# Selective scan on one core: products with C moved one unit behind their scans, and GpSimd's share of them spread from pairs to every fourth unit

## The chip, the cores and the metric

One core of a Trainium2 chip runs the whole kernel in one launch. The metric is the time of the launch on the device in microseconds (us); the number given is the median of three runs. The engines of the core are named as the profile names them: PE (TensorE; PEld is its weight load), DVE (VectorE), ACT (ScalarE), POOL (GpSimd) and SP (SyncE, which issues nearly all DMAs here).

## The reference, cut to what matters

The input is `x`, 8 images of 96 channels and 64 x 64 pixels, so 4096 tokens each. Layer 0 is a group normalisation and a Mamba block; layer 1 is linear attention (no softmax) and a feed-forward net with rounded numbers. The change touches the Mamba block's selective scan, with 192 inner channels and 16 states:

```
delta = softplus(dt @ dt_proj_w.T + dt_proj_b)
dA    = exp(delta[..., None] * A)
dBu   = delta[..., None] * Bm[:, :, None, :] * u[..., None]
h_t   = dA_t * h_{t-1} + dBu_t            # 4096 steps in order
y_t   = sum over the 16 states n of h_t[:, n] * C_t[n]
y     = (y + u * D) * silu(z);  out = y @ out_proj_w.T
```

## The kernel before, in words

**Chunks and units.** The images are worked in four pairs, each in 8 chunks of 512 tokens: 32 chunks, in order. A chunk's scan is cut into 24 units (`NU`), numbered u = 0 to 23. Eight units belong to one of three channel blocks j; within these, two units (b = 0, 1) belong to each of four groups of states g. `where(u)` gives (j, g, b). One unit covers 128 partitions and two halves h of 512 tokens.

**What a unit needs.** POOL makes dBu as `dbu` (`products_b`, L659), three units ahead (`AHEAD`; four buffers). ACT makes exp(delta A) as `da` in PSUM (`decay`, L681; two buffers), for the next unit, each half emitted right behind the scan of the same half of this unit. DVE runs two scans into `hs` (L741; three buffers of `hs`). Then `hs` is multiplied by C into `pr`. In 18 of 24 units DVE does it (L763), reading C from PSUM tile `cc`, where PE has spread it over the partitions (`rows_c`, L671; two buffers). In the six units of `POOLED` = (4, 5, 12, 13, 20, 21) POOL does it (`pooled`, L770), reading C from an SBUF tile `c`. All six have g = 2, so one load of `c` per chunk serves them: four DMAs of 128 KB, issued in unit 23 of the chunk before (`rows`, L643). Last, PE adds up the states of a pair of units into `y` (`sums`, L695), and once per block j DVE multiplies `y` by silu(z) (`gate`, L709). As the kernel before stands, the sums of the pair 20, 21 are never issued.

**What lies around the scan.** The rest of the work is cut into steps of Python generators, which a table written out by hand (`STEPS`) places in the units. `P` is the projection, convolution and delta of a later chunk, `E` the output projection, two layer norms and Gram matrix of the chunk before, `F0` and `F1` the attention and feed-forward net of a chunk 9 back, for the two images of the pair, `W` the attention's weights, `G` the group statistics of the next pair. F steps therefore run from chunk 9 on. `F1` begins in unit 8 of a chunk and has its layer norm around unit 3 of the next, so its norm meets units 2 and 3 in chunks 10 to 31.

**What sets the order.** Every engine works through its instructions in the order in which the program emits them. In `unit` that order is: POOL's product of the unit before, if it is one of `POOLED`; a copy of the last state; `rows_c` of the next unit; sums; `now("norms")`, which emits POOL's part of a layer norm (L412, L131, L132, L414) whose statistics (L406, L408) DVE made in an earlier step; the unit's first steps; `products_b`; the scans with the decays; `now("others")` (POOL's casts L1011 and others); gate; the unit's second steps; and DVE's product. `normalise` (L420, ACT) comes in the step after the norm's statistics. In unit 10 (`SILU`) ACT also makes `da` of unit 12 ahead, into other banks, and then runs two Silu over 128 x 1536 with changes of the activation table (L492, L493).

**SP.** Its DMAs go out in program order, each after the DMA eight places before it has landed. In unit 0 it spreads du and dl of block 1 over the partitions (`spread`, L634): four DMAs of 256 KB each. Around them lie the two stores of `t1d` (L883) and the load of `xr` (L822).

Of the kernel before, what the change touches and what calls it, by code (L numbers as in the profile page):

```python
# [16 lines left out]
NS = 16  # L17
NJ = 3
NG = 4
# [2 lines left out]
NK = T // 128  # L22
HID = 384
RANK = 6
POOLED = (4, 5, 12, 13, 20, 21)
POOLED_G = 2
SILU = 10
ROWS_B = (16, 18, 20, 22)
AHEAD = 3
# [36 lines left out]
def tile_mamba_linear_attention_ffn(  # L66
# [474 lines left out]
    def first_p(s, after):  # L541


        rstd, nmr = gn[0]
        xt = x_next.pop((0, 0))
        u = p1.tile([C, 2, T + 3], F32, tag="u", name="u")
        nc.scalar.activation(
            u[:, 0, :], xt[:, 0, :], AF.Identity, bias=nmr[:, 0:1], scale=rstd[:, 0:1]
        )
        nc.vector.tensor_scalar(  # L550
            u[:, 1, :], xt[:, 1, :], rstd[:, 1:2], nmr[:, 1:2], ALU.mult, ALU.add
        )
        for b in range(2):
            nc.gpsimd.memset(u[:, b, 0:3], 0.0)
        load_x(*after)
        xm = s["xm"] = p2.tile([128, NJ, T], F32, tag="xm", name="xm")
        zs = s["zs"] = p2.tile([128, NJ, T], F32, tag="zs", name="zs")
        banks = ("mp", "mE", "mF")
        for j in range(NJ):
            ps = psum(banks[j])  # L560
            for k in range(4):
                for b in range(2):
                    nc.tensor.matmul(
                        ps[64 * b : 64 * b + 64, :], lhsT=wk[:, k, 64 * j : 64 * j + 64],
                        rhs=u[:, b, k : k + T], start=(k == 0), stop=(k == 3),
                    )
            nc.scalar.activation(xm[:, j, :], ps, AF.Silu, bias=cb[:, j : j + 1])

        def proj_z(j, bank):
            ps = psum(bank)  # L570
            for b in range(2):
                nc.tensor.matmul(
                    ps[64 * b : 64 * b + 64, :], lhsT=wz[:, 64 * j : 64 * j + 64],
                    rhs=u[:, b, 3 : T + 3], start=True, stop=True,
                )
            nc.scalar.activation(zs[:, j, :], ps, AF.Silu)

        proj_z(0, "cc")
        proj_z(1, "cc")
        dbl = p1.tile([C, T], F32, tag="dbl", name="dbl")  # L580
        ps = psum("y")
        for j in range(NJ):
            nc.tensor.matmul(
                ps[0:C, :], lhsT=xpT[:, j, :], rhs=xm[:, j, :],
                start=(j == 0), stop=(j == NJ - 1),
            )
        proj_z(2, "cc")
        nc.vector.tensor_copy(dbl, ps[0:C, :])
        bd = s["bd"] = dram.tile([4 * NS, T], F32, tag="bd", name="bd")
        nc.sync.dma_start(bd, dbl[32:96, :])  # L590
        rows_b(s, 0)
        delta = p1.tile([128, NJ, T], F32, tag="delta", name="delta")
        for j in range(NJ):
            pd = psum(banks[j])
            nc.tensor.matmul(
                pd, lhsT=dtT[:, j, :], rhs=dbl[0 : 2 * RANK, :], start=True, stop=True
            )
            nc.scalar.activation(delta[:, j, :], pd, AF.Softplus, bias=dtb[:, j : j + 1])
            ld = s["ld", j] = dram.tile([128, T], F32, tag=f"ld{j}", name="ld")
            nc.scalar.dma_start(ld, delta[:, j, :])  # L600
            du = p2.tile([128, T], F32, tag="du1", name="du")
            nc.vector.tensor_mul(du, delta[:, j, :], xm[:, j, :])
            lu = s["lu", j] = dram.tile([128, T], F32, tag=f"lu{j}", name="lu")
            nc.sync.dma_start(lu, du)
            if not j:
                for to in ("du", "dl"):
                    s[to, 0] = p2.tile([128, 4, T], F32, tag=to, name=to)
                for b in range(2):
                    for n in range(NG):
                        for to, of, queue in (("du", "lu", nc.sync), ("dl", "ld", nc.scalar)):  # L610
                            queue.dma_start(
                                s[to, 0][32 * n : 32 * n + 32, 2 * b : 2 * b + 2],
                                s[of, 0].rearrange("(q e) t -> e q t", e=32)[
                                    :, 2 * b : 2 * b + 2
                                ],
                            )

        cs = s["cs"] = p2.tile([128, T], F32R, tag="cs", name="cs")
        nc.vector.tensor_copy(cs[64:96], ps[64:96, :])
        nc.vector.tensor_sub(cs[96:128], dbl[64:96], cs[64:96].bitcast(F32))  # L620
        rows_b(s, 1)
        rows(s, "c", 2 * NS, POOLED_G)
        rows_b(s, 2)
        rows_b(s, 3)

# [12 lines left out]

    def rows(s, to, of, g):

        t = s[to, g] = p2.tile([128, 2, T], F32, tag=to, name=to, bufs=NG if to == "b" else 1)
        for n in range(NG):
            nc.sync.dma_start(  # L643
                t[32 * n : 32 * n + 32],
                s["bd"][of : of + 2 * NS].rearrange("(b n) t -> n b t", b=2)[NG * g + n]
                .unsqueeze(0)
                .to_broadcast([32, 2, T]),
            )

    def rows_b(s, g):  # L650
        rows(s, "b", 0, g)

    def where(u):
        return u // (2 * NG), (u // 2) % NG, u % 2
# [8 lines left out]

    def rows_c(s, u):
        j, g, b = where(u)
        if u in POOLED:
            return
        if ("low", 0) in s:
            settle(s["low", 0])
        cc = s["cc", u] = ps_all.tile([128, T], F32, tag="cc", name="cc", bufs=2)  # L670
        nc.tensor.matmul(  # L671
            cc, lhsT=sel[64:128, g, b], rhs=s["cs"][64:128, :], start=True, stop=True
        )
# [37 lines left out]
    def unit(s, prev, nxt, first, u, steps):  # L711
        def at(v):
            return (s, v) if v < NU else (nxt, v - NU)


        if u - 1 in POOLED:
            pooled(s, u - 1)
        if u:
            nc.scalar.copy(state["new"][:, u - 1, :], s.pop(("hs", u - 1))[:, :, T - 1])  # L719
        else:  # L720
            if prev is not None:
                nc.scalar.copy(state["new"][:, NU - 1, :], prev.pop(("hs", NU - 1))[:, :, T - 1])
            state["last"] = state.get("new")
            state["new"] = p2.tile([128, NU, 2], F32, tag="state", name="state")
        to, v = at(u + 1)
        if to is not None:
            rows_c(to, v)
        if u - 3 in POOLED and u % 2 == 0:
            sums(s, u - 3)
        if u % 2 == 0 and (u or prev is not None) and (u - 1) not in POOLED:  # L730
            sums(s if u else prev, (u or NU) - 1)
        now("norms")
        steps(u, 0)
        to, v = at(u + AHEAD)
        if to is not None:
            products_b(to, v)
        hs = s["hs", u] = p2.tile([128, 2, T], F32, tag="hs", name="hs", bufs=3)
        dbu = s.pop(("dbu", u))
        to, v = at(u + 1)
        for h in range(2):  # L740
            nc.vector.tensor_tensor_scan(  # L741
                hs[:, h, :], s.pop(("da", u, h)), dbu[:, h, :],
                0.0 if first else state["last"][:, u, h : h + 1], ALU.mult, ALU.add,
            )
            if to is not None:
                decay(to, v, h)
        now("others")

        new = u % (2 * NG) == 1
        if new and u > 1:  # L750
# [6 lines left out]
        steps(u, 1)  # L757
        if new:
            skip(s, u // (2 * NG))
        if u in POOLED:  # L760
            return
        pr = s["pr", u] = p2.tile([128, 2, T], F32, tag="pr", name="pr", bufs=4)
        nc.vector.tensor_mul(  # L763
# [1 line left out]
        )  # L765

    def pooled(s, u):
        j, g, b = where(u)
        pr = s["pr", u] = p2.tile([128, 2, T], F32, tag="pq", name="pr")
        nc.gpsimd.tensor_mul(  # L770
            pr, s["hs", u], s["c", g][:, b, :].unsqueeze(1).to_broadcast([128, 2, T])
        )


# [337 lines left out]
    with tc.manual_schedule():  # L1112
# [5 lines left out]
        for i, (p, c) in enumerate(chunks):  # L1118
# [4 lines left out]
            def steps(u, part):  # L1123
                if part == 0:
                    if u in (0, 2 * NG):
                        spread(s, 1 + u // (2 * NG))
                    if nxt is not None and u == 18:
                        spread(nxt, 0)
                    if nxt is not None and u in ROWS_B:
                        rows_b(nxt, ROWS_B.index(u))  # L1130
                    if nxt is not None and u == NU - 1:
                        rows(nxt, "c", 2 * NS, POOLED_G)
                for name in (STEPS[u] + "|").split("|")[part].split():
                    step(name, i)

# [3 lines left out]
    for kind in list(waiting):  # L1139
        now(kind)  # L1140
        del waiting[kind]
    s = slots[N - 1]
    sums(s, NU - 1)
    gate(s, NJ - 1)
    rest = [(p, c, b) for p in range(NP) for c in range(NCH) for b in range(2)]
# [81 lines left out]
```

## Time and profile before

| what | value |
|---|---|
| median of 3 runs (lowest, highest) | 3166.31 us (3162.42, 3171.55) |
| span of the profiled execution | 3160.5 us |
| the median less that span | 5.8 us |
| DVE busy | 2935.2 us (93%), 4265 instructions |
| POOL busy | 2840.7 us (90%), 1921 instructions |
| PE, ACT busy | 2469.6 us (78%), 2263.9 us (72%) |
| DMA traffic | 443.75 MB, 140 GB/s on average |
| mean time from chunk to chunk, chunks 1 to 8, 10 to 30 | 88.1 us, 93.9 us |

The profile is of one execution; its span runs from the first instruction to the last, and 5.8 us of the median time lie around it. A line such as `L741 DVE TENSOR_TENSOR_SCAN hs<-da,state,dbu` names the source line, the engine, the operation, what it writes and what it reads. In a timeline the first two columns are the start and the time taken, both in us from the span's start; xN is N instructions of one kind merged, and a bracket gives the engine's idle time before and who ended it. A chunk's start is here the start of its first scan; for the chunk that starts at 1606.80 the units start at 0, 3.7, 7.8, 12.75, 16.4, 18.8 and 21.7 us after that.

### The profile page before, as it was taken

The numbers are of one execution on the slowest core, as the hardware profiler recorded it, in microseconds if no ns is written. First come the engines' busy times: TensorE is split into PE (matmuls) and PEld (weight loads), VectorE is DVE, ScalarE is ACT, GpSimd is POOL, SyncE is SP. The second block draws the span as 40 slices with busy tenths as digits, with TensorE's granted clock in tenths as the row PEclk, the third lists the DMA queues.
The fourth block names the chain that finished last, engine by engine and source line by source line (L and its number), as shares of the span: only waits on it lengthen the run. The fifth ranks groups of instructions, "written<-read, shape, count | busy, mean of one in ns | idle before, by whom it ended". The sixth has DMA issues, their size and how long they took to land. (4 is left out here: it accounts for less than half of the span.)

```text
span 3160.5 us, 35127 instructions
## 1 busy us (share of the span) xinstructions
PE 2469.6 (78%) x9450; PEld 928.7 (29%) x9450; DVE 2935.2 (93%) x4265; ACT 2263.9 (72%) x4360; POOL 2840.7 (90%) x1921
## 2 busy tenths in 40 slices
PE   6787787878787777777777778777888778887777
PEld 2122222222222223222233323222323222332344
DVE  4999999999999999999999999999999999999945
ACT  3666666667677777777777777777877777777656
POOL 2999999999999999999999999999999999999955
PEclk8677777787778888888888877898888888877668
DMA  6655556665555667555667555567565466755322
GB/s 149 152 122 137 134 156 152 160 150 135 141 143 135 138 162 175 146 129 125 141 164 170 141 146 125 137 157 170 146 148 127 124 144 162 169 132 134 95 70 73
DMA packets 253037, 443.75 MB, mean 140 GB/s; under 512 B 37605, under 2 KB 45990, under 8 KB 252838
## 3 DMA queue, kind: packets, MB, share of 16 engines
q1 hardware_dynamic: 247846, 439.40, 56.9%
q10 hardware_dynamic: 4992, 2.11, 0.3%
q8 instruction: 74, 1.21, 0.2%
q14 instruction: 125, 1.02, 0.1%
HBM read 349.11 MB, written 92.27 MB: 140 GB/s over the span
## 5 line engine op out<-in xcount | busy, mean ns | idle before, releaser
L659 POOL TENSOR_TENSOR dbu<-du,b 128x1024 f32<-128x1024 f32 x768 | 1804.6, 2371 | 112.6 <-DVE hs L741 65.5
L741 DVE TENSOR_TENSOR_SCAN hs<-da,state,dbu 128x512 f32<-128x512 f32 x1290 | 1573.5, 1265 | 25.6 <-ACT da L681 24.6
L681 ACT ACTIVATE da<-dl,aneg 128x512 f32<-128x512 f32 x1474 | 1000.6, 688 | 665.4 <-DVE hs L741 644.2
L763 DVE TENSOR_TENSOR pr<-hs,cc 128x1024 f32<-128x1024 f32 x576 | 698.7, 1213 | 35.1 <-DVE hs L741 0.5
L695 PE MATMUL y<-pr,ssum 128*32 128x512 f32 x2816 | 585.1, 831 | 113.3 <-DVE pr L763 113.3
L770 POOL TENSOR_TENSOR pr<-hs,c 128x1024 f32<-128x1024 f32 x192 | 453.8, 2363 | 36.6 <-DVE hs L741 30.4
L459 PE MATMUL mp<-u,wk 96*64 96x512 f32 x1488 | 398.1, 658 | 66.6 <-ACT xm L477 66.4
L671 PE MATMUL cc<-cs,sel 64*128 64x512 f32 x576 | 330.0, 583 | 144.8 <-DVE pr L763 144.4
L671 PEld LDWEIGHTS cc<-cs,sel 64*128 64x128 f32 x576 | 121.6, 215 | 557.3 <-DVE pr L763 296.8
L741 DVE TENSOR_TENSOR_SCAN hs<-da,dbu 128x512 f32<-128x512 f32 x184 | 213.2, 1205 | 17.4 <-POOL dbu L659 9.9
L516 PE MATMUL mp<-dbl,dtT 12*128 12x512 f32 x186 | 158.9, 947 | 56.8 <-ACT cs L506 38.5
L695 PEld LDWEIGHTS y<-pr,ssum 128*32 128x32 f32 x2816 | 87.9, 132 | 380.6 <-DVE pr L763 201.6
L791 PE MATMUL mE<-woT,zs 128*128 128x192 f32 x744 | 146.6, 350 | 66.7 <-ACT t1e L799 45.1
L459 PEld LDWEIGHTS mp<-u,wk 96*64 96x64 f32 x1488 | 97.0, 145 | 293.6 <-issue 156.6
L132 POOL TENSOR_TENSOR rs<-rs,mhalf 128x8 f32<-128x8 f32 (+1 forms) x128 | 173.3, 1354 | 10.7
L791 PEld LDWEIGHTS mE<-woT,zs 128*128 128x128 f32 x744 | 127.3, 200 | 126.8 <-ACT t1e L799 70.5
L703 PE MATMUL y<-xm,dd 128*128 128x512 f32 x192 | 129.2, 760 | 22.4 <-DVE zs L709 21.9
L467 PE MATMUL mp<-u,wz 96*64 96x512 f32 x372 | 137.0, 825 | 4.3 <-ACT xm L485 4.3
L1011 POOL CAST h<-h 128x512 fp8e5<-128x512 f16 x192 | 117.6, 622 | 24.8 <-DVE h L1003 15.8
L719 ACT COPY state<-hs 128x2 f32<-128x2 f32 x736 | 130.1, 181 | 0.2
L420 ACT ACTIVATE o<-x,nm,rs 128x96 f32<-128x96 f32 x256 | 98.6, 455 | 36.4 <-POOL nm L414 34.4
L531 POOL TENSOR_TENSOR du<-delta,xm 128x512 f32<-128x512 f32 x93 | 117.1, 1273 | 0.0
(306 smaller groups left out, 3234.1 us busy)
## 6 DMA issues: line engine op xcount, KB each, us to landing
du<-lu SPq DMA_DIRECT2D x380, 256.0 KB, 5.5
dl<-ld SPq DMA_DIRECT2D x380, 256.0 KB, 7.9
b<-bd SPq DMA_DIRECT2D x512, 128.0 KB, 5.0
lu<-du SPq DMA_DIRECT2D x96, 256.0 KB, 5.7
ld<-delta SPq DMA_DIRECT2D x93, 256.0 KB, 2.4
c<-bd SPq DMA_DIRECT2D x128, 128.0 KB, 4.4
xg<-in_x_dram SPq DMA_DIRECT2D x32, 384.0 KB, 3.8
xr<-in_x_dram SPq DMA_DIRECT2D x32, 384.0 KB, 8.7
```

What stands on the lines that cost most here:

```text
L132: nc.gpsimd.tensor_tensor(out_, out_, mhalf[0 : out_.shape[0], 0 : out_.shape[1]], op=ALU.pow)
L459: nc.tensor.matmul(ps[64 * b : 64 * b + 64, :], lhsT=wk[:, k, 64 * j : 64 * j + 64], rhs=u[:, b, k : k + T], start=(k == 0), stop=(k == 3),)
L467: nc.tensor.matmul(ps[64 * b : 64 * b + 64, :], lhsT=wz[:, 64 * j : 64 * j + 64], rhs=u[:, b, 3 : T + 3], start=True, stop=True,)
L516: nc.tensor.matmul(ps, lhsT=dtT[:, j, :], rhs=dbl[0 : 2 * RANK, :], start=True, stop=True)
L659: nc.gpsimd.tensor_mul(dbu, s["du", j][:, 2 * b : 2 * b + 2, :], s["b", g][:, b, :].unsqueeze(1).to_broadcast([128, 2, T]),)
L671: nc.tensor.matmul(cc, lhsT=sel[64:128, g, b], rhs=s["cs"][64:128, :], start=True, stop=True)
L681: nc.scalar.activation(da, s["dl", j][:, 2 * b + h, :], AF.Exp, scale=aneg[:, 2 * j + h, g : g + 1])
L695: nc.tensor.matmul(s["y"][q : q + 32, :], lhsT=ssum, rhs=pr[:, h, :], start=False, stop=(g == NG - 1),)
L741: nc.vector.tensor_tensor_scan(hs[:, h, :], s.pop(("da", u, h)), dbu[:, h, :], 0.0 if first else state["last"][:, u, h : h + 1], ALU.mult, ...
L763: nc.vector.tensor_mul(pr, hs, s.pop(("cc", u)).unsqueeze(1).to_broadcast([128, 2, T]))
L770: nc.gpsimd.tensor_mul(pr, s["hs", u], s["c", g][:, b, :].unsqueeze(1).to_broadcast([128, 2, T]))
L791: nc.tensor.matmul(ps[:, 2 * k * C : 2 * (k + 1) * C], lhsT=zs[:, j, tok : tok + 128], rhs=woT[:, j].rearrange("p b c -> p (b c)"), start= ...
```

## The change

POOL's six units per chunk become 2, 6, 10, 14, 18 and 22 (units 2 and 6 of every eight), so they are no longer neighbours. They need C of two groups (g = 1 and 3, b = 0), so the tile `c` is filled by eight DMAs of 64 KB, the four for unit 2's row first, issued in unit 1 of the chunk itself (`rows_pooled`). DVE's product of a unit (`times_c`) goes between the two scans of the next unit. `rows_c` moves from the front of the unit to behind the scans. Sums of a pair move from the even unit right behind the pair to the odd unit after that, and all twelve pairs of a chunk are summed, where there were eleven. The last unit of the last chunk gets its product behind the loop. `STEPS` is unchanged.

```
-POOLED = (4, 5, 12, 13, 20, 21)
-POOLED_G = 2
+POOLED = (2, 6)
...
-        t = s[to, g] = p2.tile([128, 2, T], F32, tag=to, name=to, bufs=NG if to == "b" else 1)
+        t = s[to, g] = p2.tile([128, 2, T], F32, tag=to, name=to, bufs=NG)
...
+    def rows_pooled(s):
+
+        t = s["c"] = p2.tile([128, len(POOLED), T], F32, tag="c", name="c", bufs=1)
+        for i, v in enumerate(POOLED):
+            _, g, b = where(v)
+            for n in range(NG):
+                row = 2 * NS + NS * b + NG * g + n
+                nc.sync.dma_start(
+                    t[32 * n : 32 * n + 32, i, :],
+                    s["bd"][row : row + 1, :].to_broadcast([32, T]),
+                )
+
+    def is_pooled(u):
+        return u % (2 * NG) in POOLED
...
-        if u - 1 in POOLED:
-            pooled(s, u - 1)
-        if u:
-            nc.scalar.copy(state["new"][:, u - 1, :], s.pop(("hs", u - 1))[:, :, T - 1])
...
+        of, v = before(1)
+        if of is not None:
+            if is_pooled(v):
+                pooled(of, v)
+            nc.scalar.copy(state["new"][:, v, :], of["hs", v][:, :, T - 1])
...
-        to, v = at(u + 1)
-        if to is not None:
-            rows_c(to, v)
-        if u - 3 in POOLED and u % 2 == 0:
-            sums(s, u - 3)
-        if u % 2 == 0 and (u or prev is not None) and (u - 1) not in POOLED:
-            sums(s if u else prev, (u or NU) - 1)
+        if u % 2:
+            far, w = before(2)
+            if far is not None:
+                sums(far, w)
         now("norms")
         steps(u, 0)
...
             if to is not None:
-                decay(to, v, h)
+                decay(to, w, h)
+            if not h and of is not None:
+                times_c(of, v)
         now("others")
+        if to is not None:
+            rows_c(to, w)
...
-        if u in POOLED:
+
+    def times_c(s, u):
+
+        hs = s.pop(("hs", u))
+        if is_pooled(u):
             return
         pr = s["pr", u] = p2.tile([128, 2, T], F32, tag="pr", name="pr", bufs=4)
...
-                    if nxt is not None and u == NU - 1:
-                        rows(nxt, "c", 2 * NS, POOLED_G)
+                    if u == 1:
+                        rows_pooled(s)
...
     s = slots[N - 1]
+    times_c(s, NU - 1)
     sums(s, NU - 1)
```

## The prediction

> **What bounds the kernel now.** I read the engines' busy shares first, then the costliest groups.
>
> ```profile
> PE 2469.6 (78%) x9450; PEld 928.7 (29%) x9450; DVE 2935.2 (93%) x4265; ACT 2263.9 (72%) x4360; POOL 2840.7 (90%) x1921
> L659 POOL TENSOR_TENSOR dbu<-du,b 128x1024 f32<-128x1024 f32 x768 | 1804.6, 2371 | 112.6 <-DVE hs L741 65.5
> L741 DVE TENSOR_TENSOR_SCAN hs<-da,state,dbu 128x512 f32<-128x512 f32 x1290 | 1573.5, 1265 | 25.6 <-ACT da L681 24.6
> L763 DVE TENSOR_TENSOR pr<-hs,cc 128x1024 f32<-128x1024 f32 x576 | 698.7, 1213 | 35.1 <-DVE hs L741 0.5
> L770 POOL TENSOR_TENSOR pr<-hs,c 128x1024 f32<-128x1024 f32 x192 | 453.8, 2363 | 36.6 <-DVE hs L741 30.4
> ```
>
> DVE sets the pace: 93% busy, and little of its idle time lies inside the chunks. Its list of waits is headed by a small row:
>
> ```profile
> DVE hs L741 <- ACT da L681: 31.7, 43, 1.2
> ```
>
> The change keeps six POOL products per chunk, so no busy time leaves DVE (or POOL); only gaps and waits can change. DVE's timeline at a chunk's start shows one gap to win:
>
> ```profile
> 1606.80 2.45 DVE L741 TENSOR_TENSOR_SCAN hs<-da,state,dbu 128x512 f32<-128x512 f32 x2
> 1609.36 1.22 DVE L763 TENSOR_TENSOR pr<-hs,cc 128x1024 f32<-128x1024 f32 x1
> 1610.49 2.45 DVE L741 TENSOR_TENSOR_SCAN hs<-da,state,dbu 128x512 f32<-128x512 f32 x2
> 1612.86 0.67 DVE L709 TENSOR_TENSOR zs<-y,zs 128x512 f32<-128x512 f32 x1
> 1613.44 1.21 DVE L763 TENSOR_TENSOR pr<-hs,cc 128x1024 f32<-128x1024 f32 x1
> ```
>
> A product right behind its own scan starts 0.11 us after it ends (1609.25 to 1609.36); behind another instruction it starts 0.09 us before that ends (1613.53 to 1613.44).
>
> **The change, part by part.** Times are from a chunk's first scan, 1606.80 here.
>
> *Product behind the next scan: -62 us.* In the trace 332 of the 576 products stand right behind their scan. Each gap of 0.10 becomes an overlap of 0.08: 332 x 0.186 = 62 us, all on DVE. The Trainium skill, "VectorE: DVE Perf Modes", section "The DRAIN you can't avoid", says that the next instruction waits for an empty pipe whatever the semaphores do. Taken so, this term would be 0 and the time 62 us higher; the rows above disagree, and I go by the rows.
>
> *Unit 14: -13 us.* In 20 chunks DVE waits 0.65 us at unit 14 for `da`. Unit 13 now holds a product, 1.13 us more cover.
>
> *Silu: +41 us.* ACT goes from the end of unit 10's second scan to unit 13's first `da` without a break:
>
> ```profile
> 1647.84 0.69 ACT L681 ACTIVATE da<-dl,aneg 128x512 f32<-128x512 f32 x1 [0.48 <-DVE hs L741]
> 1651.06 1.48 ACT L492 ACTIVATE xm<-xm 128x1536 f32<-128x1536 f32 x1
> 1655.39 1.30 ACT L681 ACTIVATE da<-dl,aneg 128x512 f32<-128x512 f32 x2
> ```
>
> That is 8.3 us (1647.80 to 1656.09). DVE has beside it the products of units 10 and 11, two pairs of scans and sometimes `G`. The product of unit 10 goes to POOL: 1.2 us of cover less. Where `G` is there its 0.55 us of slack is used up, but unit 12 also starts sooner by the gaps; I take 1.3 us x 31 chunks = 41 (bounds 20 and 50).
>
> *Gate in unit 1: about +1 us a chunk.* The last pair's sums move from the front of unit 0 to the front of unit 1, so on PE behind `P`'s convolution (1.94 us), which waits for ACT (`da`, then `xm`). Unit 0's second scan ends at 3.6, ACT at 4.9, convolution at 6.9, sums (1.07) at 7.9; the gate is due at 7.0.
>
> *C rows and the norm in unit 3: the large term.* SP and POOL before:
>
> ```profile
> 1606.10 1.92 SPq L643 DMA_DIRECT2D c<-bd  x4
> 1608.84 2.07 SPq L634 DMA_DIRECT2D du<-lu  x4
> 1611.11 1.79 SPq L634 DMA_DIRECT2D dl<-ld  x4
> 1613.86 0.31 SPq L883 DMA_DIRECT2D t1d<-tT  x1
> 1618.61 0.25 POOL L412 TENSOR_SCALAR nm<-mv 128x4 f32<-128x4 f32 x1 [2.35 <-DVE mv L408]
> 1619.24 1.04 POOL L132 TENSOR_TENSOR rs<-rs,mhalf 128x4 f32<-128x4 f32 x1
> ```
>
> The rows went out before the spread of block 1; now they go behind it and behind the second `t1d`, in one queue that lands in order. By the trace's landing times, averaged over chunks 10 to 31, the four rows land at 4.4 to 6.3, the last `dl` at 16.3 and that `t1d` at 16.8. Without the four rows ahead (2.4 us) `t1d` lands at 14.4, and four rows of half the size (0.3 each) by 15.6. An earlier or later stream moves this by about 1.3 either way; I take 15.0. POOL's product of unit 2 could start when `hs` is done, near 12; it waits 3 us more. Behind it on POOL stand unit 3's norm and casts, and ACT waits for that norm already:
>
> ```profile
> 1620.59 1.54 ACT L420 ACTIVATE o<-x,nm,rs 128x96 f32<-128x96 f32 x4 [1.01 <-POOL nm L414]
> 1622.04 1.28 ACT L681 ACTIVATE da<-dl,aneg 128x512 f32<-128x512 f32 x2
> ```
>
> Behind ACT's `normalise` stands `da` of unit 4, for which DVE waits. So: 15.0 + product 2.4 + norm 2.0 (1618.61 to 1620.55) + normalise 1.5 + `da` 0.7 = 21.6. Unit 4 started at 16.4 with four products done; with three, and three gaps won, it is due at 14.8. Delay 6.8 us, the gate's 1 us within it, in the 22 chunks with this norm: +150 us. Were the rows on time (12.0) it would start at 18.6: 3.8 x 22 = +84 even then. At 16.8 it is +189.
>
> Chunks 1 to 9 have no norm there, but `hs` has three buffers: unit 5's scan overwrites what POOL's product of unit 2 reads. Their `t1d` lands at 19.4, so the rows at about 18.2 and the product ends at 20.6. Unit 5 was due at 17.1 (17.9 before, less four gaps). With some slack in the stream I take 3.0 x 9 = +27 (9 if only the gate bites, 32 at most).
>
> The Trainium skill, "SBUF — State Buffer", section "The DMA setup-cost knee", speaks against eight small transfers: about 2 us each that does not shrink with size. Four in series would be 8.6 us by its formula, an estimate; here four rows of 128 KB land 0.6 us apart.
>
> *Later waits: -15 us.* `res` in unit 16 waits 23 us in all and `x` in unit 17 6 us, at the end of chains through POOL. POOL gains idle time from the stalls; I take half.
>
> *At nothing:* the added pair's sums (1.07 us of PE per chunk, in PE's 22% idle; 34 us if they all lay on the path); `rows_c` later by half a unit (it has a unit of slack, and its 0.5 us would show as a DVE wait for PE); pair 20, 21's tile of `pr`; POOL's other five products, which keep their number.
>
> Sum: 150 + 27 + 41 - 62 - 13 - 15 = +128 us on the profiled span of 3160.5, so 3288.5, and 5.8 around it: **3294 us**. The span plus 5.8 is the median by construction; the runs spread 0.3%, about what can be told from no change.
>
> **Rivals.** *C rows on time.* If the queue is empty earlier, the large term is 84 and chunks 1 to 9 pay 9: +44, 3210 us. For it: SP runs ahead of DVE in places. Against: from unit 18 on the queue is never empty, landing after landing.
>
> *Faster.* The norm in unit 3 stays off DVE's path: the rows land by 12, and POOL's product and norm finish before ACT comes to `normalise`. Then the terms 150 and 27 are gone: -62 - 13 - 15 + 41 = -49, 3117 us. It decides if unit 4's `da` is ready by 14.8, so if the norm is ready by 12.6. Against: ACT already waits 1.01 us for this norm without a product ahead of it.
>
> *POOL becomes the bound.* POOL is 88 us busy of 93.9 per chunk. If its 3 to 4 us wait for the rows is not made up, DVE waits for `dbu` or `hs` later too, most likely near units 18 to 21, where three du products come together: 2 us x 31 more, 3356 us.
>
> That the change is not what it says I exclude: the emitted order has each piece where the diff puts it.
>
> **How the numbers follow.** Late rows as worked out 0.65 (own range 3240 to 3345: rows at 13.7 give 121 instead of 150, at 16.8 they give 189, and the small terms are good for some 20 either way), rows on time 0.14, faster 0.14, POOL bound 0.07. The range of 8 in 10 leaves out the faster case and most of the last: 3180 to 3350. Faster by over 0.3%: the faster case, 0.14. Within 0.3%: 0.04 from the low end of rows on time. Slower: 0.82.
>
> **What the next profile would show.** Right: gaps before `pr` near 0 instead of 35.1 us; DVE's wait for `da` near 200 us instead of 31.7, most of it at unit 4; POOL's `pr` waiting for the DMA of `c`, some 3 us a chunk; ACT's wait for `nm` near 150; `zs` waiting for PE's `y` near 30. Wrong: no DMA wait on POOL's `pr`, or unit 4 starting before 16 in chunks 10 to 31.

## The result, and the profile after

The changed kernel takes 3428.57 us (median of 4 runs, 3425.25 to 3436.82) against 3165.3 us for the kernel before in runs beside it: a ratio of 1.0837, 95% interval 1.0818 to 1.0856. The direction was forecast, the size was not: +128 us were forecast on the profiled span, and the span went from 3160.5 to 3423.4 us, +263. The time lies above the given range of 3180 to 3350 us.

The page of the changed kernel, by engine and by line:

```profile
PE 2686.0 (78%) x9706; PEld 1042.9 (30%) x9706; DVE 2913.4 (85%) x4265; ACT 2254.4 (66%) x4360; POOL 2841.8 (83%) x1921
L753 DVE TENSOR_TENSOR_SCAN hs<-da,state,dbu 128x512 f32<-128x512 f32 x1290 | 1599.9, 1268 | 178.4 <-ACT da L694 165.6
L790 POOL TENSOR_TENSOR pr<-hs,c 128x1024 f32<-128x1024 f32 x192 | 452.8, 2358 | 284.6 <-DMA c<-bd 124.5
L783 DVE TENSOR_TENSOR pr<-hs,cc 128x1024 f32<-128x1024 f32 x576 | 688.0, 1194 | 0.1
L458 PE MATMUL mp<-u,wk 96*64 96x512 f32 x1488 | 499.2, 788 | 69.7 <-ACT xm L476 51.8
L419 ACT ACTIVATE o<-x,nm,rs 128x96 f32<-128x96 f32 x256 | 98.6, 455 | 114.0 <-POOL nm L413 114.0
```

DVE and POOL do the same work as before and are less busy, 85% and 83%: the time is waiting. DVE's idle time before its products fell from 35.1 to 0.1 us, as the change intends. Before its scans it rose from 25.6 to 178.4 us, POOL's products wait 284.6 us instead of 36.6, and ACT's norm waits 114.0 us for POOL instead of 34.4. The convolution on PE (L458) is the same 1488 passes, but one takes 788 ns where it took 658, on this line of the page before:

```profile
L459 PE MATMUL mp<-u,wk 96*64 96x512 f32 x1488 | 398.1, 658 | 66.6 <-ACT xm L477 66.4
```

DVE's list of waits in the changed kernel (total us, times, longest us):

```profile
DVE hs L753 <- ACT da L694: 195.9, 80, 7.8
DVE gram L888 <- PE mE L879: 64.0, 25, 4.0
DVE zs L722 <- PE y L708: 60.8, 51, 6.0
DVE res L1068 <- ACT delta L519: 39.5, 16, 3.1
```

The first row stood at 31.7 us before. The next two were hardly there:

```profile
DVE zs L709 <- PE y L695: 4.7, 4, 3.6
DVE gram L868 <- PE mE L859: 2.5, 5, 0.8
```

They are PE's, and so is the fourth in the end, since ACT's `delta` reads a product of PE.

**The late rows of C.** The large term of the forecast, in the chunk that starts at 1737.80 us; SP, POOL, ACT and DVE one below the other (SPq is SP's queue, `nm` belongs to a norm):

```profile
1743.63 0.31 SPq L903 DMA_DIRECT2D t1d<-tT  x1
1744.74 7.88 SPq L658 DMA_DIRECT2D c<-bd  x8
...
1753.34 2.34 POOL L790 TENSOR_TENSOR pr<-hs,c 128x1024 f32<-128x1024 f32 x1 [4.53 <-DMA c<-bd]
1755.77 0.25 POOL L411 TENSOR_SCALAR nm<-mv 128x4 f32<-128x4 f32 x1
...
1757.74 1.54 ACT L419 ACTIVATE o<-x,nm,rs 128x96 f32<-128x96 f32 x4 [3.58 <-POOL nm L413]
1759.19 1.28 ACT L694 ACTIVATE da<-dl,aneg 128x512 f32<-128x512 f32 x2
...
1759.96 1.28 DVE L753 TENSOR_TENSOR_SCAN hs<-da,state,dbu 128x512 f32<-128x512 f32 x1 [4.51 <-ACT da L694]
```

Read downwards, it is one chain: the eight rows are issued behind `t1d`; POOL stands 4.53 us for them; the norm is queued behind POOL's product; ACT stands 3.58 us for the norm; and behind ACT's normalise comes the `da` for which DVE stands 4.51 us at unit 4. Unit 4 starts at 22.2 us of this chunk; before, it started at 16.4.

**The clock of PE.** The same chunk, PE and then DVE (its first scan, the moved product behind it, and the gate in unit 1), and the clock granted to PE over two stretches of 3.40 us, ahead of the convolution and in it (columns: stretch, its length, busy us of PE, PEld, DVE, ACT, POOL, then PEclk, DMA share, GB/s):

```profile
1740.98 0.50 PE L684 MATMUL cc<-cs,sel 64*128 64x512 f32 x1
1742.74 3.37 PE L458 MATMUL mp<-u,wk 96*64 96x512 f32 x8 [1.26 <-ACT xm L476]
1746.05 1.27 PE L708 MATMUL y<-pr,ssum 128*32 128x512 f32 x8
```

```profile
1737.80 1.26 DVE L753 TENSOR_TENSOR_SCAN hs<-da,state,dbu 128x512 f32<-128x512 f32 x1
1738.97 1.20 DVE L783 TENSOR_TENSOR pr<-hs,cc 128x1024 f32<-128x1024 f32 x1
...
1743.57 1.28 DVE L753 TENSOR_TENSOR_SCAN hs<-da,state,dbu 128x512 f32<-128x512 f32 x1
1747.42 0.69 DVE L722 TENSOR_TENSOR zs<-y,zs 128x512 f32<-128x512 f32 x1 [2.58 <-PE y L708]
```

```profile
1739.70:1743.10 3.40, 2.14 (x12) 0.85 (x10) 3.40 (x4) 2.90 (x7) 3.40 (x2) 1.00 0.86 228
1743.10:1746.50 3.40, 3.40 (x12) 0.69 (x12) 1.75 (x2) 1.55 (x5) 3.40 (x4) 0.50 1.05 226
```

PE is busy for 2.14 of 3.40 us at full clock, with a pause of 1.26 us for ACT in it. The next stretch is at half clock, the convolution takes 3.37 us instead of 1.94, the sums behind it are late, and the gate waits 2.58 us. Over the whole span the granted clock fell from 0.807 to 0.738.

### The profile page after: what moved, and what is told of

Read it like the earlier page. It is cut to its first block, busy times and chain, and to the rows that moved or that the text cites. A ratio compares the mean times of both kernels' runs of the same rounds, so it can differ in the third digit from the quotient of the medians.

```text
span 3423.4 us, 35805 instructions
## 1 busy us (share of the span) xinstructions
PE 2686.0 (78%) x9706; PEld 1042.9 (30%) x9706; DVE 2913.4 (85%) x4265; ACT 2254.4 (66%) x4360; POOL 2841.8 (83%) x1921
## 3 DMA queue, kind: packets, MB, share of 16 engines
q8 instruction: 76, 1.25, 0.2%
## 5 line engine op out<-in xcount | busy, mean ns | idle before, releaser
L753 DVE TENSOR_TENSOR_SCAN hs<-da,state,dbu 128x512 f32<-128x512 f32 x1290 | 1599.9, 1268 | 178.4 <-ACT da L694 165.6
L790 POOL TENSOR_TENSOR pr<-hs,c 128x1024 f32<-128x1024 f32 x192 | 452.8, 2358 | 284.6 <-DMA c<-bd 124.5
L708 PE MATMUL y<-pr,ssum 128*32 128x512 f32 x3072 | 566.7, 813 | 9.9 <-POOL pr L790 9.9
L458 PE MATMUL mp<-u,wk 96*64 96x512 f32 x1488 | 499.2, 788 | 69.7 <-ACT xm L476 51.8
L684 PE MATMUL cc<-cs,sel 64*128 64x512 f32 x576 | 350.7, 609 | 171.7 <-DVE pr L783 170.9
L811 PE MATMUL mE<-woT,zs 128*128 128x192 f32 x744 | 208.2, 453 | 83.2 <-DVE x L988 48.7
L811 PEld LDWEIGHTS mE<-woT,zs 128*128 128x128 f32 x744 | 185.3, 275 | 104.0 <-DVE x L988 55.9
L716 PE MATMUL y<-xm,dd 128*128 128x512 f32 x192 | 162.8, 944 | 68.8 <-DVE zs L722 68.8
L458 PEld LDWEIGHTS mp<-u,wk 96*64 96x64 f32 x1488 | 122.8, 167 | 296.9 <-issue 197.5
L419 ACT ACTIVATE o<-x,nm,rs 128x96 f32<-128x96 f32 x256 | 98.6, 455 | 114.0 <-POOL nm L413 114.0
L466 PE MATMUL mp<-u,wz 96*64 96x512 f32 x372 | 109.0, 666 | 52.9 <-ACT zs L489 52.6
L497 PE MATMUL mp<-xm,xpT 128*96 128x512 f32 x186 | 150.4, 975 | 0.0
L1031 POOL CAST h<-h 128x512 fp8e5<-128x512 f16 x192 | 116.8, 618 | 34.1 <-DVE h L1023 15.5
```

Of the source, the lines that this page charges most:

```text
L458: nc.tensor.matmul(ps[64 * b : 64 * b + 64, :], lhsT=wk[:, k, 64 * j : 64 * j + 64], rhs=u[:, b, k : k + T], start=(k == 0), stop=(k == 3),)
L684: nc.tensor.matmul(cc, lhsT=sel[64:128, g, b], rhs=s["cs"][64:128, :], start=True, stop=True)
L708: nc.tensor.matmul(s["y"][q : q + 32, :], lhsT=ssum, rhs=pr[:, h, :], start=False, stop=(g == NG - 1),)
L716: nc.tensor.matmul(s["y"], lhsT=dd[:, j, :], rhs=s["xm"][:, j, :], start=True, stop=False)
L753: nc.vector.tensor_tensor_scan(hs[:, h, :], s.pop(("da", u, h)), dbu[:, h, :], 0.0 if first else state["last"][:, u, h : h + 1], ALU.mult, ...
L790: nc.gpsimd.tensor_mul(pr, s["hs", u], s["c"][:, i, :].unsqueeze(1).to_broadcast([128, 2, T]))
```

## The experiments

The ratios are to the kernel before in runs beside each; a gain over the changed kernel ("After") is the difference from its 3428.57 us. Waits by unit are added up from the trace's records of DVE's pauses over 0.15 us.

**The added pair of sums.** After, without the sums of units 20 and 21:

```
+            if u == 21:
+                continue
```

> The changed kernel with the sums of pair 20, 21 left out again, so eleven pairs per chunk as before. Theory A (clock): the twelfth pair makes PE's granted clock fall from 0.81 to 0.74, and slower matmuls make the gate, the Gram matrix and the residual late; then the clock comes back to 0.79 or more, DVE's waits for PE's y and mE (60.8 and 64.0 us) fall by more than half, and the time falls by 80 to 120 us, to a ratio near 1.055. Theory B (place): the waits come from where sums and C rows stand in PE's order; then the clock stays below 0.76, the waits stay, and the time falls by 10 to 35 us (the pair's own 1.07 us per chunk), ratio 1.073 to 1.08.

3429.26 us, 1.0846 (1.0827 to 1.0865): no gain, where one theory had 80 to 120 us and the other 10 to 35. The clock stays at 0.739. And the other way round, the kernel before with the twelfth pair summed in unit 0 of the next chunk:

```
+        if u == 0 and prev is not None:
+            sums(prev, NU - 3)
```

> The kernel before with nothing changed but that the sums of pair 20, 21 are issued too, in unit 0 of the next chunk. Theory A (clock): the granted clock falls from 0.81 to 0.77 or less and the time grows by 20 to 60 us. Theory B (place): the clock stays within 0.01 and the time within 10 us (1.07 us of PE per chunk in its idle time).

3165.8 us, 1.0004 (0.9995 to 1.0014). The pair costs nothing, in either kernel; that more work on PE should lower its clock falls with it.

**The two halves of the change.** First the moved products, `rows_c` and sums, with POOL's pairs and their rows as before:

```
-POOLED = (2, 6)
+POOLED = (4, 5, 12, 13, 20, 21)
...
-                    if u == 1:
-                        rows_pooled(s)
+                    if nxt is not None and u == NU - 1:
+                        rows(nxt, "c", 2 * NS, POOLED_G)
```

> The changed kernel with POOL's units put back to the pairs 4, 5, 12, 13, 20, 21 and their rows of C loaded as in the kernel before; products one unit behind their scans, the later rows_c and sums, and twelve pairs stay. If the spread of POOL's units is the main cost: no wait at unit 4, unit 13 as in the kernel before, gate and Gram matrix keep some 100 us of waits, the gaps before pr are gone (-62): near 3200 us, ratio 1.00 to 1.02. If the place of the products, sums and rows_c is the main cost: over 3300 us, ratio above 1.04.

3263.44 us, 1.0311 (1.0294 to 1.0328): +100 us, between the two expectations (about +35, and over +136). DVE's waits in this run:

```profile
DVE hs L743 <- ACT da L684: 81.7, 103, 2.4
DVE gram L878 <- PE mE L869: 64.4, 25, 3.2
DVE zs L712 <- PE y L698: 62.4, 41, 6.4
```

Both waits for PE are here at full size without the late rows. The wait for `da` is 50 us longer than before, which the expectation did not have; it grew at units 4, 13 and 15. One thing more moves in this run: the kernel before issues the sums of POOL's pairs in units 8 and 16, and here they come a unit earlier (two units in the two runs below that are built on this one). Then POOL's units 2 and 6 with their rows, put on the kernel before, with its products, `rows_c` and sums where they were:

```
-POOLED = (4, 5, 12, 13, 20, 21)
+POOLED = (2, 6)
...
-                    if nxt is not None and u == NU - 1:
-                        rows(nxt, "c", 2 * NS, POOLED_G)
+                    if u == 1:
+                        rows_pooled(s)
```

> The kernel before with POOL's units 2 and 6 of eight and the eight DMAs of C's rows in unit 1, all else as before (product right behind its scan, rows_c and sums in their old places, twelve pairs). Late rows and the norm behind the product: unit 4 at about 21.6 instead of 16.6 in chunks 10 to 31, +5 x 22 = 110 us, and Silu +37: near 3310 us, ratio 1.045. Rival (the spread alone is harmless, only with the moved products does it hurt): ratio below 1.02.

3334.85 us, 1.0544 (1.0528 to 1.056): +171, of which 118.7 us are waits at unit 4 in 22 chunks. 100 + 171 = 271, against 263 measured for both together: the two halves add up in total, but not wait by wait. At unit 13 (Silu) DVE pauses 26.6 us with the products alone and 15.5 with the spread alone, hardly more than the 16.6 before, and 58.2 with both; the +37 that was expected here did not come. And the wait for `mE` appears in both halves:

```profile
DVE gram L879 <- PE mE L870: 22.1, 16, 2.6
```

In this run `rows_c` and the sums stand in their old places (only the pairs 4, 5 and 12, 13, now no longer POOL's, are summed two units earlier), and the granted clock is 0.755 instead of 0.807: the order of the sums is not all that makes `mE` late.

**The late rows, two ways.** After, with the rows issued in unit 0 ahead of the spread instead of in unit 1:

```
+                    if u == 0:
+                        rows_pooled(s)
                     if u in (0, 2 * NG):
...
-                    if u == 1:
-                        rows_pooled(s)
```

> The changed kernel with the eight DMAs of C's rows issued in unit 0 ahead of the spread of du and dl, not in unit 1 behind it. Theory (late rows): they land by about 7 us instead of 15.0, POOL's product of unit 2 starts when its scans end (12.7), the norm behind it is ready at 17.1, unit 4 of chunks 10 to 31 starts at 19.3 instead of 22.0, POOL's wait for the DMA of c is gone, and the time falls by 2.7 x 22 = 60 us, ratio near 1.065. Rival (the norm behind the product is the whole of it, or the gate's wait takes its place): less than 25 us.

3352.89 us, 1.0605 (1.0583 to 1.0627): -76 us. The fourth row lands at 5.3 us of the chunk instead of 15.0, no POOL product waits for a row, and unit 4 starts at 19.70 us (22.04 in after). The waits for `y` and `mE` stay, 64.9 and 72.1 us. Second, the norm ahead of POOL's product:

```
+        now("norms")
         if of is not None:
             if is_pooled(v):
...
-        now("norms")
         steps(u, 0)
```

> The changed kernel with POOL's part of the layer norms emitted ahead of its product of the unit before, not behind it. Theory (late rows, norm behind them): in chunks 10 to 31 unit 4 starts near 18.4 us instead of 22.0 (statistics ready at 14.3, norm 1.95, normalise 1.45, da 0.7), ACT's 114 us wait for nm falls to some 60, and the time falls by 3.6 x 22 = 79 us, ratio near 1.059. Rival (POOL's late product then makes its casts and dbu late, and the stall only moves): unit 4 starts near 18 but the time falls by less than 25 us.

3375.09 us, 1.0673 (1.0657 to 1.0689): -53 us. The wait at unit 4 falls from 117.5 to 37.2 us, but the gate's in chunks 10 to 31 grows from 33.2 to 45.0 us; the gain lies between the two expectations (79 us, and under 25).

**The sums.** After, with the sums of a pair back in the even unit, behind the scans and `rows_c`, half a unit to a unit earlier on PE:

```
-        if u % 2:
-            far, w = before(2)
-            if far is not None:
-                sums(far, w)
...
             rows_c(to, w)
+        if u % 2 == 0 and of is not None:
+            sums(of, v)
```

> The changed kernel with the sums of a pair emitted half a unit earlier: in the even unit, behind its scans and rows of C, not at the front of the odd unit. Theory B (place): the gate's wait for y falls from 60.8 to under 10 us, the Gram matrix's wait for mE from 64 to some 40; in chunks 10 to 31 unit 4 is held by the rows anyway, so the time falls by 18 (gates of chunks 1 to 9) + 7 + 25 = 50 us, ratio near 1.068. Theory A (clock): gate and Gram waits stay above half, and the time falls by less than 25 us.

3355.65 us, 1.0611 (1.0592 to 1.0629): -73 us. The wait at the gate is gone, that for `mE` is halved, and the granted clock is 0.765 instead of 0.738. Against that unit 4 starts at 22.65 us and waits 163 us: without the gate's pause ahead of it, DVE reaches unit 4 sooner (unit 3 starts at 12.6 us instead of 14.2) and finds the same late rows.

```profile
DVE hs L749 <- ACT da L694: 237.7, 77, 10.7
DVE hs L749 <- POOL dbu L672: 35.2, 11, 11.2
DVE gram L886 <- PE mE L877: 30.7, 25, 1.9
```

All three cures together:

> The changed kernel with the three edits together: norms ahead of POOL's product, rows of C ahead of the spread, sums in the even unit behind the scans. If the waits add up: unit 4's and the gate's wait gone, the Gram matrix's wait near 10 us, Silu's +41 and the gaps' -62 stay: near 3180 us, ratio 1.00 to 1.015. If stalls only move on to later units (a lower clock of PE, late casts): above 3250 us, ratio above 1.027.

3243.34 us, 1.0256 (1.0236 to 1.0276). The three gains alone come to 53 + 76 + 73 = 202 us, together to 185. It stays between the two expectations, 80 us above before: 60.6 us of waits at unit 13 (Silu), 38.8 at unit 4, 31.4 for `mE`, 20.7 for `cc` before the products.

**The products alone, with early sums.** The edit of the sums, on the run with the moved products alone:

> The products one unit behind their scans with POOL's pairs and rows as before (the run before with that alone took 3263.4 us, 1.031), and the sums of a pair in the even unit, behind the scans and rows_c. Theory (of the +100 us, the gate's 62 and half of the Gram matrix's 64 come from sums that stand one unit late on PE; the products themselves bring their -62): DVE's wait for y before the gate under 10 us, for mE about 30, da still near 80; time 3263 - 55 - 30 = about 3178 us, 1.000 to 1.010 of before. Rival (the products behind the next scan cost by themselves, through da and the cc buffers that come free half a unit later, and the gate's wait only turns into another): over 3215 us, 1.016.

3200.28 us, 1.012 (1.0105 to 1.0135), between theory and rival. The gate's wait nearly went, but that for `mE` only fell to 52.1 us:

```profile
DVE gram L876 <- PE mE L867: 52.1, 25, 3.4
DVE res L1056 <- ACT delta L520: 9.3, 10, 1.6
PE mp L516 <- ACT cs L506: 8.9, 8, 2.1
```

DVE's pauses of over 0.15 us within the scan come to 171 us, 104 more than before: `da` 65 more (at units 4, 13 and 15), `gram` 52 more, `res` 14 less. 104 lost and 62 won make +42; the span grew by 39.

**What keeps `mE` late.** PE in units 17 to 19 of one chunk of that run:

```profile
1699.17 1.97 PE L706 MATMUL y<-xm,dd 128*128 128x512 f32 x2
1700.93 0.53 PE L935 MATMUL mF<-wff,kv 96*96 96x96 f32 x2
1702.71 0.79 PE L674 MATMUL cc<-cs,sel 64*128 64x512 f32 x1 [1.25 <-DVE pr L771]
1703.43 1.93 PE L698 MATMUL y<-pr,ssum 128*32 128x512 f32 x8
1705.29 3.17 PE L459 MATMUL mp<-u,wk 96*64 96x512 f32 x8
```

All at half clock but for the end of the last row, with a pause of 1.25 us in front of `cc`; in the 21 chunks from 10 to 30 this pause is 1.25 to 2.67 us. The next run fills it: the matmul just ahead of it is done three times, which is more work for PE.

```
-        nc.tensor.matmul(
-            s["y"], lhsT=dd[:, j, :], rhs=s["xm"][:, j, :], start=True, stop=False
-        )
+        for k in range(3):
+            nc.tensor.matmul(
+                s["y"], lhsT=dd[:, j, :], rhs=s["xm"][:, j, :], start=True, stop=k < 2,
+            )
```

> The run with the products behind the next scan and the sums in the even unit (3200.3 us; DVE waits 52.1 us for the Gram matrix mE), with the matmul that opens each accumulation of y (xm by dd) done three times instead of once, the same values: it stands in PE's queue just ahead of the 1.25 us in which PE waits in unit 18 for a free cc, and fills that gap. Adds 2.1 us of PE at full clock three times per chunk. Theory (PE's pause of 1.25 us leaves its clock at half, and at half clock the passes that follow in units 18 and 19 take twice as long and bring mE late): the wait for mE falls below 25 us, though PE does more, and the time goes to 3165 to 3190 us. Rival (mE is late because more PE work stands ahead of it, whatever the clock): the wait for mE grows beyond 52 us and the time is above 3205 us.

3196.07 us, 1.0085 (1.007 to 1.0101). The same place in this run, then two of DVE's waits and one of PE's:

```profile
1696.51 5.35 PE L707 MATMUL y<-xm,dd 128*128 128x512 f32 x6
1701.69 0.34 PE L936 MATMUL mF<-wff,kv 96*96 96x96 f32 x2
1701.96 0.49 PE L674 MATMUL cc<-cs,sel 64*128 64x512 f32 x1
1702.38 1.06 PE L698 MATMUL y<-pr,ssum 128*32 128x512 f32 x8
1703.38 1.94 PE L459 MATMUL mp<-u,wk 96*64 96x512 f32 x8
```

```profile
DVE res L1057 <- ACT delta L520: 34.9, 20, 2.8
DVE gram L877 <- PE mE L868: 23.0, 19, 2.3
```

```profile
PE mp L516 <- ACT cs L506: 45.0, 26, 2.7
```

With six passes in place of two PE goes to full clock before `cc`, and what follows takes half the time. The convolution block there takes 1.94 us in each of the 20 chunks from 10 on that have it; it took 3.27 us on average in the run without the filling, and 3.90 in the changed kernel. The granted clock rose from 0.806 to 0.844, and the wait for `mE` fell from 52.1 to 23.0 us: the theory's mechanism is shown. Its time (3165 to 3190) is missed by 6 us, since DVE's wait for `delta` grew from 9.3 to 34.9 us. That is the clock again, the other way round, and not a longer queue: no added pass stands in units 12 to 16. In units 12 and 13 of chunks 10 to 30 the granted clock is 0.97 instead of 0.72, so PE is done there 1.9 us earlier, counted from the start of unit 14, and then waits for ACT's `cs`, 45.0 us in all instead of 8.9. Behind that pause the clock of units 14 to 16 is 0.69 instead of 0.89, and PE's products for `delta` end at 13.6 us after the start of unit 14 instead of 11.9. One chunk, first without and then with the filling:

```profile
1491.56 1.12 PE L516 MATMUL mp<-dbl,dtT 12*128 12x512 f32 x2
```

```profile
1487.36 2.07 PE L516 MATMUL mp<-dbl,dtT 12*128 12x512 f32 x2 [2.06 <-ACT cs L506]
```

A cruder filling, each matmul of `rows_c` in after done twice:

```
+        for _ in range(2):
             nc.tensor.matmul(
                 cc, lhsT=sel[64:128, g, b], rhs=s["cs"][64:128, :], start=True, stop=True
             )
```

> The changed kernel with each matmul of rows_c done twice into the same bank, the same values: 576 more passes of 0.49 us at full clock, 9 us of PE per chunk. Theory (PE's clock halves where PE's short waits leave it half idle, and doubles after 3.4 us without a pause; the waits for y and mE are partly that): PE is idle less, the granted clock rises from 0.738 to over 0.77, and the waits for y (60.8 us) and mE (64.0) do not grow, so the time is within 15 us of 3428 or below. Rival (the clock follows PE's load, or doesn't matter, and PE's passes add to every chain through it): clock at or below 0.74, the waits for y and mE grow by 0.5 us and more per chunk each, time over 3445 us, 1.089.

3443.22 us (3426.5 to 3447.12), 1.0873 (1.0842 to 1.0904), clock 0.748, waits for `y` 70.7 and `mE` 70.8 us. It meets neither expectation and decides nothing: these passes stand behind the pause for a free `cc`, not in it.

**A version a little ahead of both.** The product moved in units 6 to 11 and 20 to 23 only, where no wait was seen behind the gain; POOL's pairs and rows as before, but all twelve pairs summed, and the sums of POOL's pairs in units 6, 14 and 22:

```
+OWN = (0, 1, 2, 3, 4, 5, 12, 13, 14, 15, 16, 17, 18, 19)
...
+        if v in OWN:
+            rows_c(*at(u + 1))
+            if u % 2 == 0:
+                sums(of, v)
         now("norms")
...
-            if not h and of is not None:
+            if not h and of is not None and v not in OWN:
                 times_c(of, v)
...
+        if u in OWN:
+            times_c(s, u)
```

> From the run with the products behind the next scan and the sums in the even unit (3200.3 us, 1.012): the move kept only where no wait stood behind it. The products of units 6 to 11 and 20 to 23 go behind the next scan, those of 0 to 5 and 12 to 19 stand behind their own scan, with rows_c and sums at the front of the unit as before. In the trace of before 165 of the 332 products that stand right behind their scan lie in the ten units. Theory (the move wins 0.19 us for each such product, and loses through ACT's norm at unit 4, PE's order at units 17 to 19 and ACT's Silu at unit 13 alone): 165 x 0.186 = 31 us won, 10 of them given back at unit 13, so 3145 us, 0.993 of before, DVE's waits for mE and at units 4, 14 and 15 as before. Rival (any DVE gain inside a chunk is given back by the next engine that is late): 1.000, 3162 us or more.

3160.99 us against 3170.26 beside it, 0.9972 (0.9957 to 0.9986): faster by some 9 us, where 21 were expected. DVE waits 15.4 us for `y` in six places that the expectation did not have. PE waits 52.0 us for POOL's products, which it did not before, because their sums now stand close behind them; what this costs no run separates. The 12 runs spread from 3146 to 3175 us, with the clock from 0.81 down to 0.788; the correlation of the two is -0.83.

## Why the prediction was right in direction and wrong in size

The pauses of DVE within the scan grew by 322 us (67 to 389), and 322 - 62 = 260 is the change of the span to 3 us. By the prediction's own steps:

- *Product behind the next scan, -62*: right. The idle time before `pr` went from 35.1 to 0.1 us, and the product starts 0.09 us before the scan ahead of it ends (1737.80 + 1.26 = 1739.06, and the product starts at 1738.97). The prediction took from the Trainium skill ("VectorE: DVE Perf Modes", "The DRAIN you can't avoid") only the rule of a pipe that empties before the next instruction; the same section adds that "A next op that is not held starts earlier", and an earlier start is what these rows show.
- *Unit 14, -13*: right; no wait is left there.
- *Silu, +41*: right in size. DVE's pauses at unit 13 went from 16.6 to 58.2 us, +42. The reason given, that unit 10's product goes to POOL, is not enough: with the spread alone it goes there too, and the pauses are 15.5 us. There unit 12's product, now DVE's, stands ahead of unit 13's scans; in the changed kernel it stands between them.
- *C rows and the norm in unit 3, +150 with the gate in it*: right, step by step. The fourth row lands at 15.0 us on average, as worked out, with 0.2 us between one row and the next; POOL starts at 15.4; unit 4 starts at 22.0 (21.6 forecast). DVE's waits in these chunks are 117.5 us at unit 4 and 33.2 at the gate, 150.7 together. That the sum agrees so closely has some luck in it: the gate's share was taken as 22 and came as 33.2, and a longer wait at the gate leaves a shorter one at unit 4 (163 us where the gate's is gone).
- *Gate in unit 1, +1 us a chunk*: right at full clock only. In 19 of the 30 chunks that show it the wait is 0.92 to 1.25 us. In ten others the convolution or the sums run at half clock, and it is 2.3 to 3.5 us (chunk 1, where more is late, has 5.95). The step took 1.94 us for the convolution, one duration of two.
- *Chunks 1 to 9, +27*: the stall at unit 5 did not come. Rows land at 15.8 and POOL's product starts at 16.4, earlier than the 18.2 assumed, and unit 5 starts at 19.1 behind the gate's wait and needs no buffer sooner. What came was the gate alone, 17.7 us.
- *Later waits, -15*: **this step failed.** POOL's idle time was to make them shorter. All of DVE's pauses that no step above names, nearly all of them from unit 16 on, grew by 125 us instead: `gram` and the copies of `W` beside it by 70, the scans in units 18 to 23 by 27, `res` by 18, the gate in unit 17 by 8, unit 6 by 8; `x` lost its 7. The 140 us between -15 and +125, less 9 for chunks 1 to 9, are the whole miss of 135 to within 4 us.
- *At nothing*: the added pair was rightly put at nothing. `rows_c` was put at nothing by its slack of a unit, and the later sums of the other pairs had no term but the gate; what stands behind them on PE was not asked. The Gram matrix of `E` does, and the convolution. The run with early sums shows that their place matters (`mE` 64.0 to 30.7 us, gate 60.8 to about 0), and the filled pause that a large part is clock and not order: there `mE` fell from 52.1 to 23.0 us with more work ahead of it.

So two things were left out of the sum: that PE is an in-order queue too, whose later work moves with the sums, and that its durations depend on how it pauses. Of the rivals none came true; "POOL becomes the bound" was nearest in time (3356 us) and wrong in cause, since POOL is 83% busy and DVE's wait for `dbu` grew from 9.9 to 21.5 us only. Of the signs that were named, `da` (near 200, 195.9 measured), the gaps before `pr` and POOL's wait for the rows (124.5 us, 4 a chunk) came about as stated; `zs` near 30 (60.8) and ACT's `nm` near 150 (114.0) did not.

How the 64 us of `mE` in the changed kernel divide between order and clock no run separates: the early sums change both at once. What was filled is the pause in the run with the products alone and early sums. Of the other 55 us of later waits, the early sums took `res` from 41.6 to 15.5 us and the scans in units 18 to 23 from 27.9 to 14.9; the cause of what is left there, and of the 8 us at unit 6, stays open.

## What to carry to other kernels

When an instruction is moved on an engine that is not the bound, list what is queued behind it on that engine and who waits for that; a share of idle time is no cover for it. A gain on the engine that sets the pace is worth something only up to the next wait: here 62 us were won between waits and more than that was lost in them, and moving only the products that no wait follows left 9 us. Look where a late load's consumer stands in its queue: POOL's pause of some 5 us a chunk cost DVE 118 us, because a norm that others need stood behind the product that paused.

## What the runs showed of the hardware

PE has two speeds in one run. The trace's records of the granted clock know 1.0 and 0.5 only, in spells that are multiples of 3.41 us; the same eight passes of the convolution take 1.94 or about 3.7 us. The fall from full to half comes after a stretch of 3.41 us in which PE was busy with passes or weight loads for about half of it (median 0.49 before, 0.45 in after) and the longest single pause was 1.65 and 1.75 us in the median, so pauses of one to two us are enough. The way back needs a stretch without a pause: in nine of ten cases PE was busy for all of it, and a busy stretch does not always bring it. So a small stall elsewhere makes PE wait, PE's clock halves, its work takes twice as long, and this makes the next stall. A PE that is done early does the same to itself, as the products for `delta` show in the run with the filled pause. In all, 359 of 926 such stretches were at half clock before, 527 of 1003 in the changed kernel. The Trainium skill ("TensorE: Matmul & The Clock Gate", "Part 1: The HAM clock gate (the "warmup" mystery)") has the two states and the window of 3413 ns, and these records agree. Its condition for the fall, an idle window, is stricter than what these traces show.
